# Block products of two row tiles at a time in the second matrix product, with differences of the weight made on chip

## The chip, the cores and the metric

The kernel runs on one core of a Trainium2 chip. The metric is device time in microseconds (us), the median of several executions. Five engines work side by side, each through its own queue in order: PE (matrix product; the weight loads of its array are counted apart as PEld), DVE (vector), ACT (scalar, activation), POOL (GpSimd) and SP (which here only starts DMA transfers). PE reads SBUF and writes PSUM; DVE takes results out of PSUM.

## What is computed

Two stages, each a normalisation, a quantisation and a matrix product, added to the residual (cut to what matters):

```
x = x + tanh(g_xattn) * matmul(fq(layernorm(x)), fq(ctx))     # x: 2 x 1024 x 2048, ctx: 2 x 2048 x 2048
# second stage, with h = layernorm(x)
s  = 127 / clip(max(abs(h), axis=-1), 1e-5)                   # one scale for each row
q  = clip(round(h * s), -128, 127)
sw = 1 / clip(mean(abs(weight)), 1e-5)                        # weight: 2048 x 2048
tw = clip(round(weight * sw), -1, 1)                          # -1, 0 or 1
x  = x + tanh(g_ffn) * einsum('bsi,oi->bso', q / s, tw) / sw
```

`fq` is a rounding to 256 steps. The change is in the second product, q times tw. Its left side holds whole numbers up to 128 in size, in float16; its right side holds -1, 0 and 1, in 8-bit floats. The row scales are put on when a product is taken out of PSUM, so rows with different scales can be added to each other before that.

## The kernel before

The 2 x 1024 rows are two batches of 8 row tiles of 128 rows. For each tile: `norm1` (statistics, quantisation, turning by a DMA transpose into a `turned` slot, named aT), `first` (the product with the context, two halves of 1024 columns, h = 0 and 1), `terms` (the zero-point terms of the first product, added to the residual, and the sum over the row), `norm2` (deviation, its largest square, quantisation, turning into a `turned` slot, named qT) and `second` (the product with the weight, two halves, each with a store to the output). The weight comes in once, is quantised and lies turned in `tw` for the rest of the run. Batch 1 is the end of the program: its row tiles in order of use are called rows[0] to rows[7] here, and while it runs the weight is ready.

A half tile of either product is 32 matmuls of 128 x 128 against 128 x 512, into one of three PSUM buffers of 1024 columns (`mm`). When the 32 are done, DVE multiplies the buffer by the row scale `am` and adds it to the residual `resid` (line 823; line 620 for the first product), and the half is stored (line 829), from POOL's queue, or from SP's for the two tiles in `final` (rows[6] and rows[7]).

Buffers that the change touches: `ca` holds the quantised context of the batch, 16 keys for h = 0 and h = 1 together, each of 4096 bytes a partition: keys 0 to 7 are read by `first` with h = 0, keys 8 to 15 with h = 1. `turned` has five slots (`tp`), each taken by an aT or a qT; an aT gives its slot back after `first` with h = 1 of its tile, a qT after its last product.

Nothing is issued in the order of the text. `step` notes an engine, a guessed duration, a due time, what is read and written, and what buffer is taken or given back. `Plan.give_out` lays the steps out by simulating the engines, ten times, each time with due times that are the latest starts of the round before; the order with the earliest end is issued. A step with `port=True` shares one port in that simulation, whatever its engine. So all engine queues have a fixed order, and the due times written in the code are only the starting point.

The order of batch 1's units as the code gives it:

```
order = [(t, h) for h in range(2) for t in rows[:4]]
order += [(t, h) for t in rows[4:] for h in range(2)]
```

that is, the first four tiles with h = 0, the same with h = 1, and then each of the last four with h = 0 and h = 1 together; then `second` for rows[0] to rows[7] (lines 1067 to 1092).

Of the kernel before, what the change touches and what calls it, by code (L numbers as in the profile page):

```python
# [12 lines left out]
F8 = mybir.dt.float8e4  # L13
# [160 lines left out]
def flamingo_gated_kernel(  # L174
# [104 lines left out]
    def ca_keys(slot):  # L279
        return [("ca", 2 * slot), ("ca", 2 * slot + 1)]  # L280
# [10 lines left out]

    plan = Plan({"work": NWORK, "tp": NTP, "mm": 3, "tr": 2})
    step = plan.step
    aT, qT, pm = {}, {}, {}
    taken = {}

    def scalars():
# [32 lines left out]
    def res(t):  # L330
        return resid[:, t % MT, :]
# [270 lines left out]
    def first(t, h, due):  # L602

        v = res(t)[:, ts(h, H)]

        def mult(kts, slot=None):
            if slot is not None:
                pm[t] = mm[slot]
            for kt in kts:
                for q in range(2):  # L610
                    nc.tensor.matmul(  # L611
                        pm[t][:, ts(q, U)],
                        aT[t][:, kt, :],
                        a2(kt, h * H + q * U, U),
                        start=(kt == 0),
                        stop=(kt == KT - 1),
                    )

        def add():
            nc.vector.scalar_tensor_tensor(v, pm[t], g1, v, ALU.mult, ALU.add)  # L620

        by = None
        for p in range(HB):
            last = p == HB - 1 and h == 1 and ("aT", t) in taken
            n = step(
                "PE", 0.87, due, (lambda p: lambda slot=None: mult((2 * p, 2 * p + 1), slot))(p),
                rd=[("aT", t, 2 * p // HB), ("ca", h * HB + p)] + aT_keys.get(t, []),
                wr=[("pm", t)], take=None if p else "mm", give=[taken["aT", t]] if last else [],
            )
            by = n if p == 0 else by  # L630
        step("DVE", 1.36, due - 30.0, add, rd=[("pm", t), ("g",)], wr=xk(t, h), give=[by])
# [104 lines left out]
    def norm2_tile(t, due, by_pe, by_act, ready, scales):  # L736

        s = {}
        v = res(t)
        key = lambda *a: ("n2t", t) + a

        def quant(slot):
            s["q"] = work[:, slot, :]
            nc.scalar.activation(  # L748
                s["q"].bitcast(I16).rearrange("p (k j c) -> p k j c", j=2, c=P),
                v.rearrange("p (k c j) -> p k j c", j=2, c=P),  # L750
                AF.Identity,
                bias=scales()[1],
                scale=scales()[0],
            )

        def cast():
            nc.vector.tensor_copy(s["q"], s["q"].bitcast(I16))

        def turn(h, slot):
            s["pt", h] = tr[slot].bitcast(F16).rearrange("p (c r) -> p c r", c=HB)  # L760
            for c in range(HB):
                nc.tensor.transpose(s["pt", h][:, c, :], s["q"][:, ts(h * HB + c, P)], ident)

        def copy(h, slot=None):
            if h == 0:
                s["d"] = turned[:, slot, :].rearrange("p (k r) -> p k r", k=KT)
                qT[t] = turned[:, slot, :].rearrange("p (k j r) -> p k j r", k=PB, j=2)
            (nc.scalar.copy if h < by_act else nc.vector.tensor_copy)(
                s["d"][:, ts(h, HB), :], s["pt", h]
            )  # L770

        def turn_dma(slot):
            qT[t] = turned[:, slot, :].rearrange("p (k j r) -> p k j r", k=PB, j=2)
            nc.sync.dma_start_transpose(turned[:, slot, :].rearrange("p (k r) -> p k r", k=KT), s["q"])

        by = step("ACT", 2.25, due, quant, rd=[ready] + xk(t), wr=[key("q")], take="work")
        step("DVE", 0.69, due, cast, wr=[key("q")], port=True)
        if by_pe:
            for h in range(2):
                p = step(  # L780
                    "PE", 0.5, due - 50, (lambda h: lambda slot: turn(h, slot))(h),
                    rd=[key("q")] + ([key("pt", 0)] if h else []), wr=[key("pt", h)], take="tr",
                    give=[by] if h else [],
                )
                c = step(
                    "ACT" if h < by_act else "DVE", 1.0 if h < by_act else 0.7, due - 20,
                    (lambda h: lambda slot=None: copy(h, slot))(h),
                    rd=[key("pt", h)] + ([("qT", t, 0)] if h else []), wr=[("qT", t, h)],
                    take=None if h else "tp", give=[p],
                )  # L790
                if h == 0:
                    taken["qT", t] = c
        else:
            taken["qT", t] = step(
                "SP", 1.3, due, turn_dma, rd=[key("q")], wr=[("qT", t, 0), ("qT", t, 1)], take="tp",
                give=[by], dma=3.8, port=None,
            )
# [3 lines left out]
    def second(t, h, due, parts, pool="mm", last=False, apart=False):  # L801

        n = len({q for q, _, _, _ in parts})
        lo = parts[0][0] * U
        v = res(t)[:, lo : lo + n * U]

        def mult(q, b0, b1, slot=None):
            if slot is not None:
                pm[t] = mm[slot] if pool == "mm" else tr[slot]
            o = q * U - lo  # L810
            w8 = tw_rows(q)
            for k in range(PB):
                for j in range(2):
                    nc.tensor.matmul(  # L814
                        pm[t][:, o + b0 * P : o + b1 * P],
                        qT[t][:, k, j, :],
                        w8[:, k, j, b0 * P : b1 * P],
                        start=(k + j == 0),
                        stop=(k + j == PB),
                    )  # L820

        def add():
            nc.vector.scalar_tensor_tensor(  # L823
                v, pm[t][:, 0 : n * U], am[:, t : t + 1], v, ALU.mult, ALU.add
            )

        def store():
            q = nc.sync if t in final else nc.gpsimd
            q.dma_start(out=orow[t][:, lo : lo + n * U], in_=v)  # L829

        by = None
        keys = [("xq", t, lo)] if apart else xk(t, h)
        for i, (q, b0, b1, d) in enumerate(parts):
            m = step(
                "PE", 0.865 * (b1 - b0), d,
                (lambda q, b0, b1: lambda slot=None: mult(q, b0, b1, slot))(q, b0, b1),
                rd=[("qT", t, 0), ("qT", t, 1)] + [("w", q, b) for b in range(b0, b1)], wr=[("pm", t)],
                take=None if i else pool, give=[taken["qT", t]] if last and i == len(parts) - 1 else [],
            )
            by = m if i == 0 else by  # L840
        step(
            "DVE", 0.15 + 0.61 * n, due, add, rd=[("pm", t), ("am", t)],
            wr=keys, give=[by],
        )
        step(
            "SP" if t in final else "POOL", 0.5, due, store, rd=keys, wr=[("out", t, lo)],
            dma=0.65 * n,
        )


    def weight_load(ot, place, due, queue, hold=0.0):
# [203 lines left out]
    def batch1_tiles(group):  # L1055
        dues = []
        for t in group:
            n = at[t]
            dues.append(s0_end - 45.0 + 8.0 * n if n < 4 else s0_end + 25.0 + 10.0 * (n - 4))
            load_x(t, dues[-1], "SP", hold=dues[-1] - 25.0)  # L1060
        norm1(group, dues, False, False)
# [2 lines left out]
        batch1_tiles(rows[n : n + 2])  # L1064


    due = s0_end
    order = [(t, h) for h in range(2) for t in rows[:4]]
    order += [(t, h) for t in rows[4:] for h in range(2)]
    for t, h in order:  # L1070
        first(t, h, due)
        due += 2 * UNIT
        if h == 0:
            continue
        terms(t, due)
        n = at[t]
        if n in (1, 3):
            batch1_tiles(rows[n + 3 : n + 5])
        if n in (5, 7):
            norm2(rows[n - 5 : n - 3], [due - 16.0, due - 8.0], False)  # L1080
    for n, t in enumerate(rows):
        product_scales(due - 1.0)
        for h in range(2):
            units = [(2 * h, 0, 4, due), (2 * h + 1, 0, 4, due + UNIT)]
            if h and n == MT - 1:
                second(t, h, due, units[:1], apart=True)
                second(t, h, due + UNIT, units[1:], last=True, apart=True)
            else:
                second(t, h, due, units, last=h == 1)
            due += 2 * UNIT  # L1090
        if n + 4 < MT and n % 2:
            norm2(rows[n + 3 : n + 5], [due - 16.0, due - 8.0], False)

    plan.give_out()

# [29 lines left out]
```

## Time and profile before

Three executions took 498.38, 498.38 and 499.78 us. The profiled execution took 496.74 us, with a span of 495.0 us (the recorded part).

| stretch of the span, us | PE busy | DVE busy | ACT busy | POOL busy | granted PE clock |
|---|---|---|---|---|---|
| 300 to 320 | 20.00 | 13.59 | 9.64 | 0.00 | 1.00 |
| 320 to 340 | 20.00 | 3.91 | 6.03 | 0.00 | 1.00 |
| 400 to 420 | 20.00 | 3.47 | 1.62 | 1.06 | 1.00 |
| 420 to 440 | 20.00 | 12.16 | 4.64 | 1.06 | 1.00 |
| 440 to 460 | 20.00 | 7.11 | 4.62 | 2.12 | 1.00 |
| 460 to 480 | 20.00 | 3.85 | 0.00 | 0.53 | 1.00 |
| 480 to 495 | 10.59 | 2.79 | 0.00 | 0.00 | 0.96 |

Each row is a stretch of the span and the time that each engine was at work in it. Batch 1's first product starts in pieces at 260.8 us and its last unit runs at 426.5 us; its second product starts at 373.0 us. The last matmul ends at 490.6 us, and behind it lie one addition on DVE and one store.

### The profile page before, as it was taken

The numbers are of one execution on the slowest core, as the hardware profiler recorded it, in microseconds if no ns is written. First come the engines' busy times: TensorE is split into PE (matmuls) and PEld (weight loads), VectorE is DVE, ScalarE is ACT, GpSimd is POOL, SyncE is SP. The second block draws the span as 40 slices with busy tenths as digits, with TensorE's granted clock in tenths as the row PEclk, the third lists the DMA queues.
The fourth block names the chain that finished last, engine by engine and source line by source line (L and its number), as shares of the span: only waits on it lengthen the run. The fifth ranks groups of instructions, "written<-read, shape, count | busy, mean of one in ns | idle before, by whom it ended". The sixth has DMA issues, their size and how long they took to land.

```text
span 495.0 us, 6179 instructions
## 1 busy us (share of the span) xinstructions
PE 467.6 (94%) x2422; PEld 223.0 (45%) x2422; DVE 340.6 (69%) x568; ACT 276.6 (56%) x258; POOL 63.5 (13%) x76
## 2 busy tenths in 40 slices
PE   0599999999998799999999999999999999999996
PEld 0244454444467344444444444444444444444442
DVE  4999989959999688556697957632989831572122
ACT  4997896878999988631488364530454430050000
POOL 0574529100000020100100100000000000000000
PEclk9999999999999899999999999999999999999999
DMA  8999968992189999999999995610041542215122
GB/s 293 425 419 424 366 214 338 428 407 81 60 215 366 260 301 295 306 258 330 402 363 341 297 269 189 100 28 1 0 66 47 144 111 102 86 61 153 79 92 85
DMA packets 76170, 108.94 MB, mean 220 GB/s; under 512 B 58220, under 2 KB 58220, under 8 KB 70892
## 3 DMA queue, kind: packets, MB, share of 16 engines
q1 hardware_dynamic: 72064, 93.86, 60.1%
q0 software_dynamic: 4064, 14.68, 7.7%
q8 instruction: 19, 0.31, 0.2%
q14 instruction: 11, 0.09, 0.1%
q10 hardware_dynamic: 12, 0.00, 0.0%
HBM read 77.59 MB, written 16.78 MB: 191 GB/s over the span
## 4 chain that ended last, share of the span: by engine, by line
PE 76%; DVE 14%; DMA 6%; issue 2%; ACT 1%; DVEq 0%
PE mm L814 40%; PE mm L611 32%; DVE resid L640 3%; DMA resid<-in_x_dram 2%; PE tr L814 2%; DVE strip L684 2%; DMA tw<-in_ctx_dram 2%; DVE resid L620 2%; DMA tw<-ca 2%; DVE stats L378 1%; DVE ca L550 1%; DVE ca L903 1%; ACT ca L547 1%; PE tr L444 1%; DVE colg L557 1%
## 5 line engine op out<-in xcount | busy, mean ns | idle before, releaser
L814 PE MATMUL mm<-tw,turned 128*128 128x512 fp8e4 (+1 forms) x1104 | 211.9, 353 | 4.7 <-DMA turned<-work 2.4
L611 PE MATMUL mm<-ca,turned 128*128 128x512 f16 x832 | 187.7, 384 | 0.5 <-DVE ca L550 0.3
L814 PEld LDWEIGHTS <-turned 128*128 128x128 f16 x1168 | 106.8, 98 | 122.7 <-issue 6.3
L611 PEld LDWEIGHTS <-turned 128*128 128x128 f16 x832 | 81.8, 99 | 99.0 <-issue 4.8
L823 DVE SCALAR_TENSOR_TENSOR resid<-mm,am,resid 128x1024 f32<-128x1024 f32 (+1 forms) x31 | 38.6, 1246 | 64.3 <-PE mm L814 64.2
L547 ACT ACTIVATE ca<-ca,scal 128x2048 int16<-128x2048 f32 (+1 forms) x30 | 50.5, 1692 | 36.9 <-DMA ca<-in_ctx_dram 36.4
L677 ACT ACTIVATE work<-resid,strip 128x1024 f32<-128x1024 f32 x32 | 36.4, 1138 | 57.8 <-DVE strip L668 54.1
L829 POOL DMA_DIRECT2D out_dram<-resid x30 | 18.1, 606 | 362.5 <-DVE resid L823 225.2
L620 DVE SCALAR_TENSOR_TENSOR resid<-mm,scal,resid 128x1024 f32<-128x1024 f32 x32 | 40.4, 1277 | 18.4 <-PE mm L611 18.2
L378 DVE BATCH_NORM_STATS2 stats<-resid 128x6 f32<-128x512 f32 x64 | 40.0, 678 | 7.9 <-DMA resid<-in_x_dram 7.9
L550 DVE TENSOR_SCALAR ca<-ca 128x2048 f16<-128x2048 int16 (+1 forms) x40 | 27.3, 698 | 24.5 <-ACT ca L547 24.5
L611 PE MATMUL mm<-ca,tw 128*128 128x512 f16 x192 | 43.1, 379 | 0.4 <-DVE tw L450 0.2
L748 ACT ACTIVATE work<-resid,strip 128x2048 int16<-128x2048 f32 x16 | 35.5, 2263 | 12.2 <-DVE strip L704 7.8
L684 DVE TENSOR_REDUCE strip<-work 128x1 f32<-128x1024 f32 x32 | 37.3, 1210 | 1.3 <-ACT work L677 1.3
L640 DVE SCALAR_TENSOR_TENSOR resid<-colg,rowg,resid 128x2048 f32<-128x2048 f32 x16 | 37.4, 2344 | 0.1
L434 ACT ACTIVATE work<-resid,strip 128x2048 int16<-128x2048 f32 (+1 forms) x17 | 33.4, 1984 | 1.3 <-DVE strip L400 1.3
L557 DVE TENSOR_TENSOR colg<-colg,ca 128x2048 f16<-128x2048 f16 x24 | 30.8, 1304 | 0.3
L611 PEld LDWEIGHTS <-tw 128*128 128x128 f16 x192 | 18.4, 98 | 22.8 <-DVE tw L450 0.7
L899 ACT ACTIVATE work<-ca,scal 128x2048 int16<-128x2048 f32 x13 | 25.6, 2005 | 1.6 <-DMA ca<-in_L_ffn_weight_dram 1.1
L473 ACT ACTIVATE work<-work,scal 128x2048 f16<-128x2048 f16 x8 | 16.0, 1994 | 18.5 <-DMA turned<-work 18.5
L865 ACT ACTIVATE tw<-ca 128x2048 int8<-128x2048 f32 x10 | 19.1, 1910 | 7.6 <-DMA ca<-in_L_ffn_weight_dram 7.5
L462 POOL TENSOR_TENSOR tw<-tw,work 128x512 f16<-128x512 f16 x16 | 21.8, 1364 | 1.6 <-DVE work L437 0.4
(93 smaller groups left out, 260.7 us busy)
## 6 DMA issues: line engine op xcount, KB each, us to landing
ca<-in_L_ffn_weight_dram SPq DMA_DIRECT2D x19, 1024.0 KB, 8.6
ca<-in_ctx_dram SPq DMA_DIRECT2D x16, 1024.0 KB, 12.3
resid<-in_x_dram SPq DMA_DIRECT2D x15, 1024.0 KB, 11.7
out_dram<-resid POOLq DMA_DIRECT2D x26, 512.0 KB, 3.8
tw<-in_ctx_dram SPq DMA_DIRECT2D x8, 1024.0 KB, 12.6
ca<-in_ctx_dram SPq DMA_DIRECT2D x14, 512.0 KB, 8.4
tw<-in_L_ffn_weight_dram SPq DMA_DIRECT2D x6, 1024.0 KB, 6.8
out_dram<-resid SPq DMA_DIRECT2D x3, 512.0 KB, 2.6
```

What stands on the lines that cost most here:

```text
L378: nc.vector.bn_stats(stats6[:, t % 4, c, :], res(t)[:, ts(c, 512)])
L434: nc.scalar.activation(d, v, AF.Identity, bias=bi, scale=sc)
L547: nc.scalar.activation(a.bitcast(I16), s["w"], AF.Identity, bias=zc2, scale=rs2)
L557: nc.vector.tensor_add(r, r, a2(kt - kt % 2, h * H, 2 * H))
L611: nc.tensor.matmul(pm[t][:, ts(q, U)], aT[t][:, kt, :], a2(kt, h * H + q * U, U), start=(kt == 0), stop=(kt == KT - 1),)
L620: nc.vector.scalar_tensor_tensor(v, pm[t], g1, v, ALU.mult, ALU.add)
L640: nc.vector.scalar_tensor_tensor(v, colg, rowg[:, t : t + 1], v, ALU.add, ALU.add, accum_out=acc[:, i : i + 1])
L677: nc.scalar.activation(s["dev", t, h], res(t)[:, ts(h, H)], AF.Square, bias=s["nm"][:, j : j + 1], accum_out=s["s2"][:, k : k + 1],)
L684: nc.vector.tensor_reduce(s["m2"][:, k : k + 1], s["dev", t, h], AX.X, ALU.max)
L748: nc.scalar.activation(s["q"].bitcast(I16).rearrange("p (k j c) -> p k j c", j=2, c=P), v.rearrange("p (k c j) -> p k j c", j=2, c=P), AF. ...
L814: nc.tensor.matmul(pm[t][:, o + b0 * P : o + b1 * P], qT[t][:, k, j, :], w8[:, k, j, b0 * P : b1 * P], start=(k + j == 0), stop=(k + j == PB),
L823: nc.vector.scalar_tensor_tensor(v, pm[t][:, 0 : n * U], am[:, t : t + 1], v, ALU.mult, ALU.add)
```

## The change

The tiles of batch 1 are taken in pairs for the second product. The first pair goes as before, through `second`. The other three go through a new function, `seven`: the pair's q is seen as four blocks (a11, a12 of the pair's first tile t, a21, a22 of its second tile u, each 128 rows by 1024) and the weight as four (b11 to b22, 1024 by 1024), and the four result blocks are made out of seven block products in place of eight, after Winograd. A block product is 16 matmuls of the same shape as before, in two groups of 8 (512 columns each); a pair has 7 x 16 = 112 of them where four half tiles had 128. For this, sums and differences of the blocks are needed:

- s1 = a21 + a22, s2 = s1 - a11, a11 - a21 (written over a21), s4 = a12 - s2: four steps on DVE for each pair, 128 x 1024 in float16.
- t0 = b12 - b11, t1 = b22 - t0, t2 = b22 - b12, t3 = b21 - t1 (`weight_differences`, once): 8-bit floats, 8192 a partition and block. t0, t1 and t2 are made on POOL, in 16 instructions of 512 each, t3 on DVE in 8 instructions of 1024.

The four t blocks are written over keys 0 to 7 of `ca`, s1, s2 and s4 over keys 8 to 13 (two keys for a pair). Products accumulate in PSUM over each other, and each result block is put together in `resid` by seven takes for a pair (line 823's operation), where `second` has four. `order` now has h = 0 of rows[4] to rows[7] ahead of h = 1 of the same tiles; keys 0 to 7 of `ca` are read for the last time by h = 0 of rows[7]. `norm2` of the later tiles is asked for pair by pair, and the last half tile, which was split in two units with a store each, is now the last block product, split the same way.

The diff:

```diff
--- before.py
+++ after.py
@@ -291,7 +291,7 @@
 
     plan = Plan({"work": NWORK, "tp": NTP, "mm": 3, "tr": 2})
     step = plan.step
-    aT, qT, pm = {}, {}, {}
+    aT, qT, pm, flat = {}, {}, {}, {}
     taken = {}
 
     def scalars():
@@ -770,7 +770,8 @@
             )
 
         def turn_dma(slot):
-            qT[t] = turned[:, slot, :].rearrange("p (k j r) -> p k j r", k=PB, j=2)
+            flat[t] = turned[:, slot, :]
+            qT[t] = flat[t].rearrange("p (k j r) -> p k j r", k=PB, j=2)
             nc.sync.dma_start_transpose(turned[:, slot, :].rearrange("p (k r) -> p k r", k=KT), s["q"])
 
         by = step("ACT", 2.25, due, quant, rd=[ready] + xk(t), wr=[key("q")], take="work")
@@ -846,6 +847,164 @@
             "SP" if t in final else "POOL", 0.5, due, store, rd=keys, wr=[("out", t, lo)],
             dma=0.65 * n,
         )
+
+    HK = PB // 2
+
+    def w_part(q, k):
+
+        o = (HOME[q] * PB + k * HK) * 2 * U
+        return tw.bitcast(F8)[:, o : o + HK * 2 * U]
+
+    def t_part(i, q):
+        o = (2 * i + q) * HK * 2 * U
+        return ca.bitcast(F8)[:, o : o + HK * 2 * U]
+
+    def t_key(i, q):
+        return ("ca", 2 * i + q)
+
+    def moving(v):
+        return v.rearrange("p (k o j) -> p k j o", k=HK, j=2)
+
+    def weight_differences(dues, engines):
+
+        for i, (due, by) in enumerate(zip(dues, engines)):
+            for q in range(2):
+                b11, b12, b21, b22 = w_part(q, 0), w_part(q + 2, 0), w_part(q, 1), w_part(q + 2, 1)
+                pair = ((b12, b11), (b22, t_part(0, q)), (b22, b12), (b21, t_part(1, q)))[i]
+                rd = [("w", q + 2 * n, o) for n in range(2) for o in range(4)]
+                rd += [t_key(i - 1, q)] if i == 1 else [t_key(1, q)] if i == 3 else []
+                w = HK * 2 * U // PIECES[by]
+                for c in range(PIECES[by]):
+
+                    def go(i=i, q=q, by=by, pair=pair, at=ts(c, w)):
+                        eng = nc.vector if by == "DVE" else nc.gpsimd
+                        eng.tensor_tensor(
+                            t_part(i, q)[:, at], pair[0][:, at], pair[1][:, at], ALU.subtract, saturate=False
+                        )
+
+                    step(
+                        by, w * (1.05e-3 if by == "DVE" else 2.35e-3) + 0.1, due, go, rd=rd, wr=[t_key(i, q)],
+                        port=True,
+                    )
+
+    PIECES = {"DVE": 4, "POOL": 8}
+    ENGINES = ("POOL", "POOL", "POOL", "DVE")
+
+    def seven(pair, i, due, last):
+
+        t, u = pair
+        half = HK * 2 * P
+        s = {}
+        s1, s2, s4 = (ca[:, (8 + 2 * i) * 2 * H + n * half :][:, 0:half] for n in range(3))
+        keys = [("S", i, n) for n in range(4)]
+
+        def sums(n):
+            if n == 0:
+                nc.vector.tensor_add(s1, flat[u][:, 0:half], a22())
+            elif n == 1:
+                nc.vector.tensor_sub(s2, s1, a11())
+            elif n == 2:
+                nc.vector.tensor_sub(flat[u][:, 0:half], a11(), flat[u][:, 0:half])
+            else:
+                nc.vector.tensor_sub(s4, a12(), s2)
+
+        qt, qu = [("qT", t, 0), ("qT", t, 1)], [("qT", u, 0), ("qT", u, 1)]
+        need = (qu, qt + keys[:1], qt, qt + keys[1:2])
+        put = (
+            [keys[0]] + ca_keys(4 + i), [keys[1]], [keys[2], ("qT", u, 0)], [keys[3]],
+        )
+        for n in range(4):
+            step("DVE", 0.75, due, lambda n=n: sums(n), rd=need[n], wr=put[n], port=True)
+
+        def mult(y, a, b, q, start, slot=None):
+            if slot is not None:
+                s[y] = mm[slot]
+            a = a().rearrange("p (k j r) -> p k j r", k=HK, j=2)
+            for k in range(HK):
+                for j in range(2):
+                    nc.tensor.matmul(
+                        s[y][:, ts(q, U)], a[:, k, j, :], moving(b(q))[:, k, j, :],
+                        start=start and k + j == 0, stop=k + j == HK, skip_group_check=not start,
+                    )
+
+        first_of = {}
+
+        def product(y, a, b, rd, due, start=False, qs=(0, 1), give=()):
+            for q in qs:
+                m = step(
+                    "PE", 1.73, due, lambda slot=None, q=q: mult(y, a, b, q, start, slot),
+                    rd=rd(q) + [("pm", i, y, 0)] * q, wr=[("pm", i, y, q)], take="mm" if start and q == 0 else None,
+                    give=give if q == 1 else (),
+                )
+                if start and q == 0:
+                    first_of[y] = m
+
+        def take(y, r, h, due, give=False, q=None):
+
+            v = res(r)[:, ts(h, H)] if q is None else res(r)[:, h * H + q * U :][:, 0:U]
+            w = slice(0, H) if q is None else slice(q * U, (q + 1) * U)
+
+            def add():
+                nc.vector.scalar_tensor_tensor(v, s[y][:, w], am[:, r : r + 1], v, ALU.mult, ALU.add)
+
+            parts = (0, 1) if q is None else (q,)
+            wr = xk(r, h) if q is None else [("xq", r, q)]
+            step(
+                "DVE", 1.38 if q is None else 0.8, due, add, rd=[("pm", i, y, n) for n in parts] + [("am", r)],
+                wr=wr, give=[first_of[y]] if give else [],
+            )
+            return wr
+
+        def store(r, h, keys, due, q=None):
+            lo, w = (h * H, H) if q is None else (h * H + q * U, U)
+
+            def go():
+                e = nc.sync if r in final else nc.gpsimd
+                e.dma_start(out=orow[r][:, lo : lo + w], in_=res(r)[:, lo : lo + w])
+
+            step(
+                "SP" if r in final else "POOL", 0.5, due, go, rd=keys, wr=[("out", r, lo)], dma=1.3 * w / H,
+            )
+
+        W4 = lambda q, n: [("w", q + 2 * n, o) for o in range(4)]
+        a11 = lambda: flat[t][:, 0:half]
+        a12 = lambda: flat[t][:, half : 2 * half]
+        a22 = lambda: flat[u][:, half : 2 * half]
+        tk = lambda n: lambda q: [t_key(n, q)]
+        d = 3.46
+        product("y", a11, lambda q: w_part(q, 0), lambda q: qt + W4(q, 0), due, start=True)
+        take("y", t, 0, due + d)
+        product("x", a12, lambda q: w_part(q, 1), lambda q: qt + W4(q, 0), due + d, start=True)
+        store(t, 0, take("x", t, 0, due + 2 * d, give=True), due + 2 * d)
+        product("y", lambda: s2, lambda q: t_part(1, q), lambda q: [keys[1]] + tk(1)(q), due + 2 * d)
+        take("y", t, 1, due + 3 * d)
+        product("z", lambda: s1, lambda q: t_part(0, q), lambda q: [keys[0]] + tk(0)(q), due + 3 * d, start=True)
+        take("z", u, 1, due + 4 * d)
+        product(
+            "y", lambda: flat[u][:, 0:half], lambda q: t_part(2, q), lambda q: [keys[2]] + tk(2)(q), due + 4 * d,
+        )
+        store(u, 1, take("y", u, 1, due + 5 * d), due + 5 * d)
+        product("z", lambda: s4, lambda q: w_part(q + 2, 1), lambda q: [keys[3]] + W4(q, 1), due + 5 * d)
+        store(t, 1, take("z", t, 1, due + 6 * d, give=True), due + 6 * d)
+        give = [taken["qT", t], taken["qT", u]]
+        for q in range(2):
+            product(
+                "y", a22, lambda q: t_part(3, q), lambda q: qu + tk(3)(q), due + 6 * d, qs=(q,), give=give,
+            )
+            if last:
+                store(u, 0, take("y", u, 0, due + 7 * d, q == 1, q), due + 7 * d, q)
+        if not last:
+            store(u, 0, take("y", u, 0, due + 7 * d, True), due + 7 * d)
 
 
     def weight_load(ot, place, due, queue, hold=0.0):
@@ -1064,32 +1223,35 @@
         batch1_tiles(rows[n : n + 2])
 
 
+    SEVEN = 3
     due = s0_end
-    order = [(t, h) for h in range(2) for t in rows[:4]]
-    order += [(t, h) for t in rows[4:] for h in range(2)]
+    order = [(t, h) for g in (rows[:4], rows[4:]) for h in range(2) for t in g]
     for t, h in order:
+        n = at[t]
         first(t, h, due)
         due += 2 * UNIT
+        if h == 0 and n in (1, 3):
+            batch1_tiles(rows[n + 3 : n + 5])
         if h == 0:
             continue
         terms(t, due)
-        n = at[t]
-        if n in (1, 3):
-            batch1_tiles(rows[n + 3 : n + 5])
         if n in (5, 7):
             norm2(rows[n - 5 : n - 3], [due - 16.0, due - 8.0], False)
-    for n, t in enumerate(rows):
+    s1 = due
+    weight_differences([s1 + 20.0, s1 + 30.0, s1 + 40.0, s1 + 50.0], ENGINES)
+    for n in range(0, MT, 2):
+        pair = rows[n : n + 2]
         product_scales(due - 1.0)
-        for h in range(2):
-            units = [(2 * h, 0, 4, due), (2 * h + 1, 0, 4, due + UNIT)]
-            if h and n == MT - 1:
-                second(t, h, due, units[:1], apart=True)
-                second(t, h, due + UNIT, units[1:], last=True, apart=True)
-            else:
-                second(t, h, due, units, last=h == 1)
-            due += 2 * UNIT
-        if n + 4 < MT and n % 2:
-            norm2(rows[n + 3 : n + 5], [due - 16.0, due - 8.0], False)
+        if n >= MT - 2 * SEVEN:
+            seven(pair, n // 2 - MT // 2 + SEVEN, due, n == MT - 2)
+            due += 7 * UNIT
+        else:
+            for t in pair:
+                for h in range(2):
+                    second(t, h, due, [(2 * h, 0, 4, due), (2 * h + 1, 0, 4, due + UNIT)], last=h == 1)
+                    due += 2 * UNIT
+        if n + 4 < MT:
+            norm2(rows[n + 4 : n + 6], [due - 16.0, due - 8.0], False)
 
     plan.give_out()
```

## The prediction

> **What bounds the kernel now.** I read the chain of work that ended last first, in order of time, for its end:
>
> ```profile
> 404.90 4.53 PE mm L814 x21
> 409.44 3.45 PE mm L611 x16
> 412.89 13.81 PE mm L814 x64
> 426.70 1.73 PE mm L611 x8
> 428.43 62.17 PE mm L814 x288
> 490.60 0.03 issue
> 490.63 0.75 DVE resid L823
> ```
>
> Columns are start, length and what ran. From 169 us on, the chain is PE alone, without a hole, and only the last addition and its store lie behind it. So the end moves with PE's matmuls, one for one, as long as PE always finds work. The price of one is 62.17 / 288 = 0.2159 us. Next, the stretches of the last part, for the room on the other engines (PE, PEld, DVE, ACT, POOL busy, then the granted clock):
>
> ```profile
> 340.00:360.00 20.00, 20.00 (x94) 9.10 (x93) 16.99 (x21) 4.96 (x9) 0.00 (x0) 1.00 0.00 1
> 360.00:380.00 20.00, 20.00 (x95) 9.10 (x93) 18.45 (x31) 11.47 (x15) 0.00 (x0) 1.00 0.33 53
> 380.00:400.00 20.00, 20.00 (x95) 9.00 (x94) 15.32 (x34) 9.80 (x11) 1.60 (x3) 1.00 0.43 133
> ```
>
> PE is full at full clock; POOL is nearly idle; DVE is at 85 to 92% up to 380 us, and the table of the stretches shows that it has room before 340 and after 400. Last, POOL's additions early in the run, the only ones there are, by group and then in time, with DVE beside them:
>
> ```profile
> L462 POOL TENSOR_TENSOR tw<-tw,work 128x512 f16<-128x512 f16 x16 | 21.8, 1364 | 1.6 <-DVE work L437 0.4
> ...
> 51.98 2.38 POOL L462 TENSOR_TENSOR tw<-tw,work 128x512 f16<-128x512 f16 x2
> ...
> 79.50 2.13 POOL L460 TENSOR_TENSOR tw<-work 128x512 f16<-128x512 f16 x1
> 81.71 4.12 POOL L462 TENSOR_TENSOR tw<-tw,work 128x512 f16<-128x512 f16 x2
> ...
> 79.17 3.54 DVE L557 TENSOR_TENSOR colg<-colg,ca 128x2048 f16<-128x2048 f16 x2
> 83.24 1.57 DVE L555 TENSOR_TENSOR colg<-ca 128x2048 f16<-128x2048 f16 x1
> 84.73 2.17 DVE L557 TENSOR_TENSOR colg<-colg,ca 128x2048 f16<-128x2048 f16 x1
> ```
>
> The same 512 elements take POOL 1.2 us alone and 2.1 us beside DVE additions that read two operands from SBUF; DVE's own additions take 1.57 to 2.17 us there, and 1.23 us at 294 us with POOL idle. The two hold each other up.
>
> **What it takes away.** Three pairs lose 16 matmuls each: 48 x 0.2159 = 10.36 us of PE, in the stage that sets the end. Shape and type of the matmuls stay, so I keep the price; the weight loads (98 ns each) stay hidden under matmuls of 216 ns, and without that cover 336 loads would cost up to 33 us. If PE finds work throughout, its last matmul ends at 490.60 - 10.36 = 480.2 instead of 490.6.
>
> **When W's differences must be there.** Back from 480.2: a seven-product pair is 112 x 0.2159 = 24.2 us, three are 72.5, so the first begins at 407.7. Its products are 3.45 us each. t1 is read by its third (414.6), t0 by its fourth (418.1), t2 by its fifth (421.5, the second 512 columns at 423.2), t3 by its seventh (428.4). Before 407.7 lie the first pair in the old way (27.6) and h = 1 of rows[4] to rows[7] (27.6): h = 0 of these tiles must be over at 352.5. Its last unit begins at 345.6 and frees the first key of `ca` after 4 matmuls, at 346.4: POOL starts there, and it frees keys faster than POOL fills them. t0, t1 and t2 then have 76.8 us.
>
> **Cost of t0, t1 and t2.** 3 x 16 = 48 instructions. No row has POOL writing 8-bit floats; the nearest is the 512-element float16 addition. Bounds by instruction: 0.67 us, if bytes counted (the 256-element form at its quickest), and 2.02 us, the longest of line 462, under steady collision. I take 1.23 alone, start to start at 52 us, and a collision term. From 79.50 to 85.83 POOL made three pieces in 6.25 us, 2.80 more than three times 1.15, beside 5.85 us of two-operand DVE work: 0.48 us lost for each us of it. In the new stretch that work is at most eight `terms` (2.35 each, two SBUF operands: 18.8), t3 (9.6, below), the sums of one pair (2.6) and six casts (4.1): 35.1 us, so 16.8 lost. Add four stores that POOL must issue for the first pair (0.53 each, 2.1): 48 x 1.23 + 16.8 + 2.1 = 77.9, so POOL is done at 424.3, **1.1 us late**. At 0.67 it would be 42 us early, which gains nothing; at 2.02 it ends at 346.4 + 97.0 + 2.1 = 445.5, 22.3 late. A mean of 1.364, as under DVE's full load early in the run, gives 414.0, in time. I put 1.1 into the sum, as the choice near the unfavourable middle. Stores queued behind pieces may leave later; nobody waits for them but the end, and the last pair's go by SP.
>
> The Trainium skill has a rule against this (Advanced Engine Details and Errata, GPSIMD Details): POOL shares a read and a write interface with DVE and conflicts with two-SBUF-input and two-port DVE work. The rows above agree that it conflicts, but show about half the time lost, not all. If all 35.1 us stopped POOL, it would end at 346.4 + 59.0 + 35.1 + 2.1 = 442.6, 19.4 late, and the total would be 498.38 - 10.36 + 19.4 = 507.4.
>
> **What DVE gains in work.** t3: 8 instructions of 1024. Not shown; bounds are 0.61 (half the 1.23 us addition of 2048 float16) and 1.28 (float32 of 1024 with PSUM). The reductions of 1024 single elements take 1.21, and I take 1.2: 9.6 us, needed by 428.4 and possible from t1 on, some 50 us after 346.4. Sums: 4 x 0.65 x 3 pairs (half of 1.23, plus a little; at float32 rate 1.28) = 7.8. Takes: 7 x 3 - 4 x 3 = 9 more at 1.28 = 11.5. Together 29 us in 340 to 480, where 80 of 155 us are busy now: not on the path in sum. Beside POOL DVE's two-operand work is some 55% longer (the three of line 557 above: 5.71 / 3 = 1.90 against 1.23), which I come to in the rivals. Cost taken: 0.
>
> **Takes between products.** A product that accumulates onto a PSUM buffer waits until DVE has read it. One other product (3.45) covers the take (1.28): 2.17 us are spare, four times a pair. Cost taken 0; if another DVE step of 2.35 us has just begun, 0.2 to 0.4 us; with the cover gone 1.3 each.
>
> **Order, tail, queues.** h = 0 of rows[5] to rows[7] now needs their aT at 332 to 346. Before, the last three aT transposes are issued at 314.5 and take to 322, so the aTs are early enough, if the five slots come free: four hold aTs until h = 1 and one is left for qT of rows[0] until rows[4] is over at some 359. The first pair's qTs came at 364.6 to 369.4 and are wanted at 380.1: no cost. The last 512 columns end as before in 0.75 us and a 256 KB store; the other 256 KB store now starts 1.7 us ahead of it instead of some 5: 0 to 1.3 us (half of the 2.6 us a 512 KB store takes to land), I take 0.2.
>
> **Sum.** 496.74 - 10.36 + 1.1 + 0.2 = 487.7 for an execution like the profiled one. The median of the runs is 1.64 above the profiled, and these microseconds are not PE's, so I add them: **489.3 us**. Its own range is 487 to 492.
>
> **Rivals.**
>
> *GpSimd's t2 sets the end.* The differences come late and PE stands at the fifth product of the first seven-product pair. For: 8-bit output is not in any row, and collision can double a piece. Against: the mean of 1.364 under a DVE more loaded than here. With stores, PE begins to wait at (76.8 - 2.1) / 48 = 1.56 us a piece and all 10.36 us are given back at 1.77; above that the kernel is slower. At 1.9 it is 346.4 + 91.2 + 2.1 = 439.7, 16.5 late: 498.38 - 10.36 + 16.5 + 0.2 = 504.7. Chance 0.21.
>
> *Takes come late.* While norm2 of rows[4] to rows[7] is still in DVE's queue (first two pairs, eight accumulations), two steps of 2.35 and 1.21 ahead of a take pass the 2.17 spare by 1.4. Four of eight: 5.6 us, 493.6. Against: after 440 us DVE is at 20 to 35%. Chance 0.13.
>
> *A hole ahead of the first pair.* POOL slows `terms` and the casts of rows[0] to rows[3] (4 x 55% of 2.35, and 4 x 0.31, by which line 550 is longer early in the run, 996 ns in the mean against 0.69 us alone: 6.4 us) just where DVE is at 92%; the spare is 380.1 - 373.0 = 7.1. If one slot more is late by a transpose (4.9), 4.0 us are lost: 492. Against: DVE is idle for 16 us in 320 to 340, and terms could move there. Chance 0.06.
>
> *The change doesn't do what it says.* 48 matmuls are gone but the fixed order leaves as much PE idle, in many small waits: 497 to 500. Against: PE has no hole in 320 us now. Chance 0.07, of which 0.05 within the bound and 0.02 slower.
>
> **How the numbers follow.** The forecast has 0.53. A change of under 0.3% (1.5 us) can't be told from none. Faster: 0.53 + 0.13 + 0.06 = 0.72; same 0.05; slower 0.21 + 0.02 = 0.23. The range starts at 486.8 (no late piece, and an execution 0.4 above the profiled one's 496.74 - 10.36 = 486.4) and goes to 502, which leaves out the GpSimd cases above that and a few below.
>
> **What would show it.** Right: some 48 fewer matmuls in the second product; PE busy without a hole to 480; t0 to t2 done by 424, pieces at 1.3 to 1.6 us. Wrong: PE idle in front of the fifth product with POOL as releaser (price), idle in front of third to seventh products with DVE as releaser (takes), or idle at 375 to 385 with a transpose or `am` as releaser (hole).

## The result, and the profile after

The changed kernel takes 505.23 us (median) against 498.38: a ratio of 1.0137, with a 95% interval of 1.0100 to 1.0173. It is slower, where 489.3 was forecast. The profiled execution took 505.08 us, its span 503.3.

The chain of work that ended last, around the place where it leaves PE in the last third and at its end:

```profile
352.44 0.99 DVE strip L690
353.45 1.02 DVE strip L691
354.47 1.06 DVE strip L692
...
358.71 1.03 DVE strip L368
359.77 1.03 DVE strip L703
...
363.86 1.67 DVE work L757
365.53 1.20 DVE resid L620
366.73 0.04 issue
366.78 23.44 PE mm L611 x100
...
434.06 64.06 PE mm L935 x296
498.15 0.75 DVE resid L958
```

Before, this chain was PE alone from 169 us. Now it runs through DVE for over 20 us ahead of 366.78, and most of the links are steps on two or four columns (L690 to L693, L366 to L368, L703 to L709: the small arithmetic of norm2), nearly all about 1.02 us long. Once the seven-product pairs run alone, from 434 us, PE has no hole, and 296 matmuls take 64.06 us, 0.2164 each: the shape's price did stay. Who PE waited for after 165 us (total, times, longest):

```profile
PE mm L611 <- DVE resid L620: 7.2, 1, 7.2
PE mm L815 <- DMA tw<-ca: 4.2, 2, 3.1
PE mm L815 <- DMA turned<-work: 2.1, 1, 2.1
PE mm L935 <- DVE resid L824: 1.4, 1, 1.4
PE mm L935 <- DVE resid L958: 0.8, 1, 0.8
PE mm L815 <- DVE resid L824: 0.8, 1, 0.8
```

and the stretches that answer to those shown of before:

```profile
340.00:360.00 20.00, 19.62 (x91) 8.82 (x90) 18.79 (x26) 8.88 (x11) 12.97 (x13) 1.00 0.00 1
360.00:380.00 20.00, 13.22 (x54) 5.69 (x54) 10.04 (x9) 4.33 (x2) 20.00 (x19) 0.83 0.12 26
380.00:400.00 20.00, 20.00 (x95) 9.04 (x94) 19.27 (x31) 9.39 (x11) 10.23 (x7) 1.00 0.41 80
```

Between 360 and 380 us PE makes 54 matmuls where it made 95; it stands for 7.2 us, and then its granted clock is low (the mean of the stretch is 0.83): 54 x 0.2159 = 11.7 us of work take 13.2. POOL is busy all the time there. Its differences, by form (shortest/median/longest in ns):

```profile
L891 POOL TENSOR_TENSOR ca<-tw x32: 1083/1090/1111, 347.0 to 426.0; 128x512 fp8e4<-128x512 fp8e4 x32
L891 POOL TENSOR_TENSOR ca<-tw,ca x16: 1089/1092/3145, 362.8 to 384.7; 128x512 fp8e4<-128x512 fp8e4 x16
```

POOL is not slow at all: 1.09 us a piece almost throughout, 1.06 from start to start where the forecast's sum took 1.23, and t2's last piece, the one feared, is not what PE waits for. POOL is still done only at 427.1 us, not at 424.3: twice its pieces stood for some 10 us (9.8 and 10.9) behind a store in its queue that waited for DVE. PE, late itself by then, did not wait for that.

So there are two losses of different kinds: holes in PE around 170 to 220 us, in batch 0, which the change does not touch (4.2 + 2.1 us against 2.3 before), and the hole at 360 us with its low clock and the small waits behind it. PE starts 720 matmuls after 330 us and ends at 498.1; at 0.2159 each they leave 12.7 us lost. The same count for the kernel before leaves 0.2.

### The profile page after: what moved, and what is told of

It is laid out like the page before. It is cut to its first block, busy times and chain, and to the rows that moved or that the text cites. A ratio compares the mean times of both kernels' runs of the same rounds, so it can differ in the third digit from the quotient of the medians.

```text
span 503.3 us, 6176 instructions
## 1 busy us (share of the span) xinstructions
PE 459.5 (91%) x2374; PEld 217.0 (43%) x2374; DVE 387.5 (77%) x597; ACT 275.6 (55%) x258; POOL 118.5 (24%) x124
## 4 chain that ended last, share of the span: by engine, by line
PE 39%; DMA 23%; DVE 16%; ACT 11%; issue 8%; SPq 3%; POOL 0%; DVEq 0%; ACTq 0%; POOLq 0%
PE mm L611 14%; PE mm L935 13%; PE mm L815 11%; DMA ca<-in_L_ffn_weight_dram 6%; DMA ca<-in_ctx_dram 6%; DMA turned<-work 5%; DMA tw<-ca 4%; DVE resid L640 3%; DVE strip L684 3%; ACT ca L547 3%; DMA out_dram<-resid 2%; SPq L1076 2%; ACT work L434 2%; ACT tw L1024 2%; DVE resid L620 1%
## 5 line engine op out<-in xcount | busy, mean ns | idle before, releaser
L815 PE MATMUL mm<-tw,turned 128*128 128x512 fp8e4 (+1 forms) x720 | 130.7, 341 | 7.7 <-DMA tw<-ca 4.2
L611 PEld LDWEIGHTS <-turned 128*128 128x128 f16 x832 | 81.4, 99 | 110.1 <-issue 15.0
L815 PEld LDWEIGHTS <-turned 128*128 128x128 f16 x784 | 69.1, 99 | 80.9 <-issue 10.5
L830 POOL DMA_DIRECT2D out_dram<-resid x22 | 13.5, 614 | 219.6 <-DVE resid L824 183.2
L958 DVE SCALAR_TENSOR_TENSOR resid<-mm,am,resid 128x1024 f32<-128x1024 f32 (+1 forms) x22 | 27.0, 1233 | 29.3 <-PE mm L935 29.3
L891 POOL TENSOR_TENSOR ca<-tw 128x512 fp8e4<-128x512 fp8e4 x32 | 34.0, 1091 | 58.2 <-PE mm L611 58.2
L640 DVE SCALAR_TENSOR_TENSOR resid<-colg,rowg,resid 128x2048 f32<-128x2048 f32 x16 | 43.9, 2750 | 0.2
L748 ACT ACTIVATE work<-resid,strip 128x2048 int16<-128x2048 f32 x16 | 35.3, 2248 | 12.9 <-DVE strip L704 10.7
L824 DVE SCALAR_TENSOR_TENSOR resid<-mm,am,resid 128x1024 f32<-128x1024 f32 x18 | 23.0, 1279 | 21.8 <-PE mm L815 21.8
L550 DVE TENSOR_SCALAR ca<-ca 128x2048 f16<-128x2048 int16 (+1 forms) x40 | 24.8, 640 | 6.2 <-ACT ca L547 6.2
L935 PEld LDWEIGHTS <-turned 128*128 128x128 f16 x192 | 18.8, 98 | 24.2 <-issue 1.7
## 6 DMA issues: line engine op xcount, KB each, us to landing
resid<-in_x_dram SPq DMA_DIRECT2D x15, 1024.0 KB, 11.1
```

The source lines that it names most:

```text
L611: nc.tensor.matmul(pm[t][:, ts(q, U)], aT[t][:, kt, :], a2(kt, h * H + q * U, U), start=(kt == 0), stop=(kt == KT - 1),)
L640: nc.vector.scalar_tensor_tensor(v, colg, rowg[:, t : t + 1], v, ALU.add, ALU.add, accum_out=acc[:, i : i + 1])
L748: nc.scalar.activation(s["q"].bitcast(I16).rearrange("p (k j c) -> p k j c", j=2, c=P), v.rearrange("p (k c j) -> p k j c", j=2, c=P), AF. ...
L815: nc.tensor.matmul(pm[t][:, o + b0 * P : o + b1 * P], qT[t][:, k, j, :], w8[:, k, j, b0 * P : b1 * P], start=(k + j == 0), stop=(k + j == PB),
L891: eng.tensor_tensor(t_part(i, q)[:, at], pair[0][:, at], pair[1][:, at], ALU.subtract, saturate=False)
L935: nc.tensor.matmul(s[y][:, ts(q, U)], a[:, k, j, :], moving(b(q))[:, k, j, :], start=start and k + j == 0, stop=k + j == HK, skip_group_ch ...
```

## The experiments

Three theories were set against each other. **P**: POOL's pieces hold a port that DVE's steps with two SBUF operands also need; DVE comes late, and PE with it. **O**: the new order of batch 1's units makes the holes. **V**: DVE simply has too much work. A fourth, **E**, came out of the first four runs. Each ratio is to the kernel before, with its 95% interval; the edits are to the changed kernel.

**Width of POOL's pieces taken away.** Every queue keeps its order and its number of instructions; each POOL piece writes 8 columns of its 512.

```diff
-                    def go(i=i, q=q, by=by, pair=pair, at=ts(c, w)):
+                    def go(i=i, q=q, by=by, pair=pair, at=slice(c * w, c * w + (w if by == "DVE" else 8))):
```

> Leaves out most of t0, t1 and t2: each of POOL's 48 pieces writes 8 of its 512 columns; every engine's order is the changed kernel's. Theory P (POOL's pieces hold the port and DVE's steps with two SBUF operands wait for them): DVE's two-column steps fall from about 1.02 us back to 0.16, the 7.2 us hole in PE at 360 us and its low clock (about 1.9 us) go, and most of the 3.0 us of small waits at 419 to 434: 493 to 497 us. Theory O (the new order of batch 1 and the re-laid plan make the holes): 503 to 506. Theory V (DVE simply has too much work, with or without POOL): 502 to 506.

Measured: 495.37 us, ratio 0.9908 (0.9861 to 0.9956). The two-column steps, in order of time (start, length):

```profile
353.40 0.17 DVE L690 TENSOR_TENSOR strip<-strip 128x2 f32<-128x2 f32 x1
353.61 0.20 DVE L691 TENSOR_SCALAR strip<-strip 128x2 f32<-128x2 f32 x1
353.72 0.17 DVE L692 TENSOR_TENSOR strip<-strip 128x2 f32<-128x2 f32 x1
353.92 0.16 DVE L693 SCALAR_TENSOR_TENSOR strip<-strip 128x2 f32<-128x2 f32 x1
```

They are back at 0.17, and PE has no wait at all after 330 us. What it still waits for lies in batch 0:

```profile
PE mm L815 <- DMA turned<-work: 4.6, 1, 4.6
PE mm L815 <- DMA tw<-ca: 3.2, 1, 3.2
```

With the same orders and the same number of POOL instructions, their width alone is worth 1.0137 - 0.9908 = 0.0229, or 11.4 us. P is right for the late loss; O and V are wrong for it. What the runs show is the waiting beside POOL's wide pieces; that a port is the reason is P's reading of it. But the gain is not the full 10.36 us either: something early is left.

**The same pieces, cut in four.** Each POOL step issues four instructions of 128 columns.

```diff
+                        n = 1 if by == "DVE" else 4
+                        for m in range(n):
+                            at = slice(c * w + m * w // n, c * w + (m + 1) * w // n)
```

> Same steps and orders as the changed kernel, each POOL piece of 512 issued as four instructions of 128. Theory P, if a waiting DVE step gets the port at the end of a POOL instruction: two-column steps wait some 0.3 to 0.4 us in place of 0.85, the hole at 360 us shrinks from 7.2 to 1 to 3 us, POOL's own work grows from 51 to 65 to 75 us; 498 to 502. Theories O and V: 504 to 508.

Measured: 510.36 us, ratio 1.0245 (1.0167 to 1.0323). The steps shrank as P says, to about the length of one smaller POOL instruction, and the hole at 360 us went; but another step of two columns, later, did not get through between the instructions. DVE first, then POOL:

```profile
351.42 0.34 DVE L691 TENSOR_SCALAR strip<-strip 128x2 f32<-128x2 f32 x1
352.16 0.33 DVE L693 SCALAR_TENSOR_TENSOR strip<-strip 128x2 f32<-128x2 f32 x1
...
411.69 0.54 DVE L708 SCALAR_TENSOR_TENSOR am<-strip,scal 128x2 f32<-128x2 f32 x1
412.26 11.93 DVE L709 TENSOR_TENSOR am<-am,strip 128x2 f32<-128x2 f32 x1
424.12 1.27 DVE L824 SCALAR_TENSOR_TENSOR resid<-mm,am,resid 128x1024 f32<-128x1024 f32 x1
```

```profile
412.30 11.88 POOL L894 TENSOR_TENSOR ca<-tw 128x128 fp8e4<-128x128 fp8e4 x32
424.12 0.58 POOL L830 DMA_DIRECT2D out_dram<-resid  x1
```

L709 waits until all 32 POOL instructions are over, the take behind it (L824) waits for L709, and PE stands for 13.5 us. So the forecast of this run was right on the step and wrong on the time: a waiting DVE step mostly gets in at the next end of a POOL instruction, but not always. What tells the two apart I could not find. POOL's own work grew to 88 us, where 65 to 75 were expected.

**All four differences on DVE.**

```diff
-    ENGINES = ("POOL", "POOL", "POOL", "DVE")
+    ENGINES = ("DVE", "DVE", "DVE", "DVE")
```

> All four differences on DVE (24 more steps of 1024, 1.21 us each, 29 us more on DVE), none on POOL; the plan is laid anew. Theory P: no step with two SBUF operands is longer than alone, no hole at 360 us; 493 to 500. Theory V: DVE has more work, so PE waits longer for it: above 506. Theory O: holes stay where they are, 503 to 506.

Measured: 496.12 us, ratio 0.9956 (0.9916 to 0.9996). DVE has 29 us more to do, and PE waits for it 1.1 us in all, once, long before the differences. V is wrong for three pairs. The one large hole is again early, 11.3 us behind the weight's DMA transposes.

**The new order of batch 1 alone.**

```diff
-    SEVEN = 3
+    SEVEN = 0
...
-    weight_differences([s1 + 20.0, s1 + 30.0, s1 + 40.0, s1 + 50.0], ENGINES)
```

> The new order of batch 1 alone: no differences, no seven-product pairs; PE's order is the changed kernel's for about the first 300 us. Theory P: the first 300 us cost what they cost in the changed kernel (about 5 us more than before at 235 us), nothing after that: 501 to 504. Theory O: also holes at 360 and 420 us: 508 to 514. If the early 5 us are chance of one execution: 498 to 499.

Measured: 505.46 us, ratio 1.0118 (1.0030 to 1.0205): some 6 us lost without any of the new work, between the figures of P and of O. But its trace has no hole after 330 us, where O put two. PE takes the same tiles in the same order as in the changed kernel for over 300 us. Compared with the kernel before, queues differ long before batch 1: `Plan` lays out the whole program by latest starts, so a new tail gives new due times to the weight's and batch 0's steps too. On SP, for instance, the three DMA transposes of batch 0's later qTs (line 775) are now issued in a row, where one of them had a load in front of it. This is theory **E**: not batch 1's order costs, but the other order that the plan gave to the early part.

**The early order held.** On each engine, the 793 steps that both programs build first (up to batch 1's first two pairs) are chained in the order that the plan of the kernel before gave them; the rest is planned as before.

```diff
-    ROUNDS = 10
+    ROUNDS = 10; EARLY = {"SP": [...], "DVE": [...], "ACT": [...], "PE": [...], "POOL": [...]}
...
-        waits = list(waits)
+        waits, behind = self.early(waits)
...
-            ends[n] = end
+            ends[n] = end; self.issued(n, behind, waits, open_)
...
+def _early(self, waits):
+    waits, behind = list(waits), {}
+    for line in self.EARLY.values():
+        for a, b in zip(line, line[1:]):
+            behind[a] = b
+            waits[b] += 1
+    return waits, behind
+def _issued(self, n, behind, waits, open_):
+    if n in behind:
+        m = behind[n]
+        waits[m] -= 1
+        if not waits[m]:
+            open_[self.steps[m][0]].append(m)
```

First with the new order of batch 1 alone (as in the run above):

> The order before for the early steps, and the new order of batch 1 alone: no differences, no seven-product pairs. Theory E: the new order of batch 1's units costs nothing by itself, ratio 0.997 to 1.003. If that order is what costs: ratio 1.010 to 1.015, as in the run with the new order and a new plan.

Measured: 499.33 us, ratio 1.0039 (1.0010 to 1.0068), 0.8% below the same kernel without the held order. That is just above E's 0.997 to 1.003 and clear of the rival's 1.010 to 1.015, so batch 1's order costs about 2 us by itself, 3.4 at the most. The intervals with and without the held order overlap. Then with the change itself:

> The changed kernel with one thing held: on every engine, the steps that exist in both kernels up to batch 1's first two pairs keep the order that they have in the kernel before. Theory E (the plan, laid anew for the whole program, put batch 0 and the weight in an order that costs about 6 us there): 6 us less than the changed kernel, ratio to before 1.000 to 1.006, with the hole of 5 to 15 us from POOL after 340 us still there. If the early loss belongs to something else: ratio 1.012 to 1.016 as in the changed kernel.

Measured: 503.79 us, ratio 1.0082 (1.0034 to 1.0130). The early holes are gone (1.4 us behind the weight's transposes, none behind a qT's) and most of what is lost comes after 330 us, 5.8 and 2.5 us of it in two waits for line 620. The step down from 1.0137 is 2.7 us where 6 were expected; the two intervals overlap, so this pair alone doesn't settle it, and the next one does. By the same count as above the late loss is 11.4 us. The profiled execution was the fastest of its kind, 497.07 us; where the others lose 6.7 us more at the median, no trace shows.

**The early order, and all differences on DVE.** Both edits together:

> The order before for the early steps, and all four differences on DVE. Theories P and E together: nothing of the 10.36 us is lost, ratio 0.978 to 0.984 (487.5 to 490 where before has 498.4). If E is wrong: ratio 0.992 to 0.998, as with all on DVE in the new plan.

Measured: 487.83 us, ratio 0.9786 (0.9754 to 0.9818): the whole of the 10.36 us. Its chain of waits, from the early part to the end, and two of its stretches:

```profile
198.99 34.69 PE mm L815 x160
233.69 3.45 PE tr L815 x16
237.14 31.08 PE mm L815 x144
...
317.43 62.16 PE mm L611 x288
...
411.53 69.08 PE mm L935 x320
480.61 0.02 issue
480.64 0.75 DVE resid L958
```

```profile
340.00:360.00 20.00, 20.00 (x94) 9.02 (x93) 18.82 (x39) 11.28 (x9) 0.00 (x0) 1.00 0.12 27
420.00:440.00 20.00, 20.00 (x94) 9.11 (x93) 19.90 (x25) 2.58 (x5) 2.12 (x4) 1.00 0.22 89
```

PE is full up to its last matmul at 480.6, 0.4 us behind the time that the forecast had worked out, with DVE at 91 to 99% from 340 to 440 us.

This run and the one with all differences on DVE in the new plan (0.9956) are one edit apart, the early order: 0.0170, or 8.5 us, with intervals that don't touch. The other two pairs give less, 3.9 us (batch 1's order alone) and 2.7 us (the change itself), with intervals that overlap. The traces agree that the early part is where the difference lies. PE's row for 169 to 330 us (length, PE busy, granted clock, and the DMAs) is, in this order, for the kernel before, for this run, for the changed kernel and for all differences on DVE in the new plan:

```profile
169.00:330.00 161.00, 160.69 (x737) 0.99 0.96 274
169.00:330.00 161.00, 160.43 (x743) 1.00 0.91 272
169.00:330.00 161.00, 157.25 (x712) 0.98 0.95 273
169.00:330.00 161.00, 149.87 (x688) 0.97 0.95 269
```

PE is idle there for 0.3 us before and for 0.6 to 3.2 us in all seven runs with the held order, those below included; it is idle for 3.8 us in the changed kernel, and for 6.3, 5.1 and 11.1 us in the first three runs. So E holds; its size, 3 to 9 us by the pairs, does not come out more exactly. With the changed kernel's early order (the change itself, the short and the split pieces) PE stands at 219 to 222 us for a qT's transpose, for 2.1, 4.6 and 4.2 us; in the kernel before and in the three runs so far with its early order it does not.

**A wait for POOL.** The early order held, and POOL's pieces given a key that norm2 of rows[2] and rows[3] writes:

```diff
+                rd += [("n2", rows[2], "f")] if by == "POOL" else []
```

> The order before for the early steps, and three differences on POOL as in the change, but POOL's pieces wait until DVE has the quantisation scales of rows[2] and rows[3] (about 350 us). Theory P: no chain of two-column steps of 1.02 us ahead of 360 us and no hole there; what is left are the chains of rows[4] to rows[7] and the four terms beside POOL: PE loses 2 to 8 us after 340, ratio 0.985 to 0.998. If the hole is not the port's doing: ratio 1.000 to 1.006, as without the wait.

Measured: 507.17 us, ratio 1.0165 (1.0112 to 1.0218), a miss, and the trace shows why: the key orders the plan and nothing on the chip. POOL began when its data was free, and the plan had now put two norm2 groups behind each other there:

```profile
346.23 15.83 POOL L892 TENSOR_TENSOR ca<-tw 128x512 fp8e4<-128x512 fp8e4 x15 [68.60 <-PE mm L611]
```

```profile
347.36 1.04 DVE L690 TENSOR_TENSOR strip<-strip 128x2 f32<-128x2 f32 x1
348.44 1.02 DVE L691 TENSOR_SCALAR strip<-strip 128x2 f32<-128x2 f32 x1
...
400.83 8.85 DVE L368 SCALAR_TENSOR_TENSOR strip<-strip 128x4 f32<-128x4 f32 x1
409.71 0.17 DVE L703 TENSOR_SCALAR strip<-strip 128x2 f32<-128x2 f32 x1
```

Two chains beside POOL in place of one made a hole of 9.8 us in place of 5.8 with the early order alone (7.2 in the changed kernel). That fits P; whether a real wait would have helped was not tried. L368 is another step that waited for a whole run of pieces.

**One block on POOL.** Early order, `ENGINES = ("DVE", "DVE", "POOL", "DVE")`.

> As the run with the early order and all differences on DVE, but t2 alone (16 of 48 pieces) on POOL. Theory P: POOL's 17 us still meet DVE's steps; each two-operand step beside it waits to the end of a piece, a third of the three-block loss at the most: 1 to 6 us more than all on DVE, ratio 0.981 to 0.991. If POOL's volume is what hurts and not where it falls: ratio 0.984 to 0.986. If a single block is harmless: 0.977 to 0.981.

Measured: 491.05 us, ratio 0.9866 (0.9815 to 0.9916). Now POOL's 16 pieces meet DVE's own pieces of the other blocks:

```profile
349.92 27.33 POOL L891 TENSOR_TENSOR ca<-tw 128x512 fp8e4<-128x512 fp8e4 x16 [74.21 <-PE mm L611]
```

```profile
358.85 8.08 DVE L891 TENSOR_TENSOR ca<-tw 128x1024 fp8e4<-128x1024 fp8e4 x4
366.85 1.27 DVE L620 SCALAR_TENSOR_TENSOR resid<-mm,scal,resid 128x1024 f32<-128x1024 f32 x1
```

Long two-operand streams take turns: POOL takes 1.71 us a piece in the mean in place of 1.06, DVE 2.02 in place of 1.22. PE waits 1.3 us for the take behind them. The ratio is 4 us worse than with all on DVE, but the intervals overlap a little, and the profiled execution, 487.54 us, took no longer than the other's 487.55. So that one block on POOL costs 4 us is not shown; it gives nothing back either.

**How many pairs.** Early order, all on DVE, `SEVEN = 4`:

> Early order, all differences on DVE, and seven products for all four pairs: 13.8 us of matmuls less than before. If PE's matmuls still set the end: ratio 0.971 to 0.975. Theory V (DVE, at 95% between 340 and 440 us with three pairs, sets the end): t1 and t2 come late for the first pair, ratio 0.985 to 1.010.

Measured: 493.87 us, ratio 0.9932 (0.9898 to 0.9967). PE now waits for DVE, at 391 to 395 us and again at 425 to 429 us:

```profile
PE mm L935 <- DVE ca L891: 3.4, 3, 1.7
PE mm L935 <- DVE resid L958: 1.7, 1, 1.7
```

V is right from the fourth pair on. And `SEVEN = 2`:

> Early order, all differences on DVE, seven products for the last two pairs only: 6.9 us of matmuls less than before. If each pair is worth its 16 matmuls of 0.2159 us and nothing else: ratio 0.984 to 0.988, 3.5 us above three pairs. If DVE's work was still in the way with three pairs: the same time as with three.

Measured: 493.75 us, ratio 0.9942 (0.9902 to 0.9982), above the 0.984 to 0.988 of the forecast. Its profiled execution, 492.3 us, has no hole after 330 us and its last matmul ends at 485.4, 4.8 us behind three pairs' for 16 matmuls (3.5 us): the late part is as expected, and the early part, on the same orders, was 1.2 us later. The ratios lie 0.0156 apart, 7.8 us; the 3 us of that which the two profiled executions don't show stay open. Three pairs is the best of those tried.

## Why the prediction was wrong, point by point

**Right.** The bound: PE's matmuls set the end, and 48 fewer of them are worth 10.36 us if PE finds work (10.7 us measured, 0.0214 of 498.38, or 9.1 to 12.3 by the interval, with its last matmul at 480.6 where 480.2 was worked out). The price of a matmul stayed. t3 and the sums were sized well: 1.21 us for 1024 8-bit elements (1.2 taken), 0.68 for a sum (0.65 taken). Takes between products did cost little: 3.0 us in the changed kernel, behind DVE steps that POOL had held up (L640 with 8.18 us, L917 with 3.95), and none with all differences on DVE. The slots of `turned` and the aTs held nothing up.

**Wrong: the step "Cost of t0, t1 and t2".** It saw the collision and charged it to POOL: "0.48 us lost for each us", 16.8 us, and t2 1.1 us late. So the sum had nothing for a delay of DVE, where the width of POOL's pieces cost 11.4 us. The rows that it read were float16 additions of POOL beside DVE's. In the new stretch POOL's 8-bit pieces took 1.06 us from start to start and lost 2 us in each of two pieces (3.14), beside `terms`; the rest of the loss was DVE's. The prediction's count of what collides was wrong too: it listed terms, t3, sums and casts, 35.1 us by length, and left out norm2's steps on two or four columns without a word. By number they matter most: nearly each takes 0.16 us alone and about 1.02 beside POOL, whatever its work, since it waits for a piece to end (now and then two get through behind one piece: 0.95 and 0.15 us in the run with the added key). Twelve in a row, 2.5 us with the short pieces, took 11.6.

**Wrong: the rival "A hole ahead of the first pair".** It had the right engine and nearly the right place, 360 us, but priced it by the longer steps (6.4 us, under a spare of 7.1; with a transpose of 4.9 more, 4.2 us lost by its own terms and not 4.0) and gave it 0.06. Its buffer was wrong as well: PE stopped not for qT or `am` of the first pair, but for the takes of the *first* product (line 620), which stood in DVE's queue behind norm2 and held the PSUM buffers.

**Wrong: taking everything ahead of the change as fixed.** The sum let the first 300 us stand, and the argument "PE has no hole in 320 us now" was taken as evidence for the new plan. All queues of this kernel come out of one plan for the whole program, and a new tail moved batch 0's steps: 2.7, 3.9 and 8.5 us in the three pairs of runs, the last alone clear of noise.

Together: the change measured +6.85 us. Going from the kernel before to it by way of two runs, that is -10.7 (both losses out) + 6.1 (from there to the run with short pieces and the new plan) + 11.4 (width of POOL's pieces). Such steps add up whatever their causes, so the sum proves nothing. The middle step holds the early order, but also POOL's short pieces in place of DVE's work; the pairs above are the better measure of the early order. Which of the early steps makes the loss, beyond the transpose at 219 us, was not taken apart.

## What to carry to other kernels

When work is moved to GpSimd, count the instructions, not the microseconds, of DVE work beside it: a chain of tiny steps with two SBUF operands paid up to one GpSimd instruction each here, and what stood behind that chain in DVE's queue paid for all. Where one planner orders a whole program, hold the order of the part that a change doesn't touch before judging the change: here that was worth some 3 to 9 us, where 10.36 were looked for. And an idle engine is not a reason to give it work: DVE, at 91 to 99% but with POOL idle beside it, did all four blocks for three pairs without delaying PE.

## What the hardware showed that I had not expected

- An 8-bit subtraction of 512 columns on POOL takes 1.09 us (1.06 from start to start), where the float16 addition of the same size took 1.15 at its quickest; it hardly yields to DVE's steps with a few columns.
- Not only steps with two tensor operands wait beside POOL: L691, a float32 step with one tensor and constants, takes 1.02 us too. L668 (the same operation on one column, 0.14), L360 (reciprocal), the reductions and the takes out of PSUM keep their lengths. The Trainium skill (Advanced Engine Details and Errata, Mode Summary) says that GpSimd's instructions and DVE's two-port ones block each other. L691's 1.02 us agrees with that if L691 ran in such a mode, which no run here shows.
- Some waits last for a whole run of POOL instructions: 11.93 us (L709), 8.85 (L368) and 8.18 (L640, alone 2.35). Most end with the piece that is running. The cause is open.
- After PE's hole of 7.2 us the granted clock was low: 0.83 over 360 to 380 us, some 1.6 us on top of the hole. The run with four pairs has the same 0.83 over 420 to 440 us, where PE waited for 2.7 us.
